# Graph filter convolution on one core: places of the sorted chunks, the engine that writes the early bias, and the step in which a sorted chunk's store is issued

## The chip, the core and the metric

The kernel runs on one NeuronCore of a Trainium2 chip. The metric is the device time of one execution in microseconds (us). The core's engines run their own instruction streams side by side and wait for each other through semaphores: TensorE (PE, with its weight loads as PEld), VectorE (DVE), ScalarE (ACT), GpSimd (POOL) and SyncE (SP). In this kernel SP issues the plain DMAs and POOL the indirect ones.

## The reference

There are 12,500 nodes with 128 features and 412,500 edges, sorted by their destination. Cut to what matters:

```python
h = jnp.maximum(_layernorm(x, axis=-1), 0.0)
h = h @ W_in2f
Wij = ssp(f_ij @ W_f1 + b_f1) @ W_f2 + b_f2          # ssp(x) = softplus(x) - log 2
Wij = Wij * rcut_ij[:, None]
x_ij = h[idx_j] * Wij                                 # idx_j = dst, sorted
agg = jax.ops.segment_sum(x_ij, idx_i, num_segments=h.shape[0])   # idx_i = src, not sorted
out = ssp(agg @ W_o1 + b_o1) @ W_o2 + b_o2
return x + out
```

For each edge a small network of two layers makes a filter of 128 numbers from 20 edge features; the filter, scaled by the edge's cutoff, is multiplied with the row of `h` at one end of the edge, and the products are added up at the other end.

## The kernel before

**Chunks and steps.** The edges are worked in 806 chunks of 512, each with four tiles of 128 edges; four chunks form a group. The main loop runs one `step(k)` (L1521) per chunk, software-pipelined: each step has a list of parts, and a part works for a chunk some steps ahead or behind. The order of the parts is the string `ORDER`, written by hand; since every engine takes its instructions in the order in which they are issued, this string sets the order on each engine:

```python
ORDER, FIRST_ORDER = "EMTBCKHVSPIWJZRLU", "MTBHVPWENISLJZRU"
```

What the parts that matter here do in step k:

- E (`hidden_end`, L875, DVE): ends the first filter layer of chunk k+2; it reads what ACT's last two activations of that layer made.
- M (`message`, L1047 and L1048, DVE): `o` = filter times picked rows, for chunk k. Then the scatter of the chunk before is issued.
- T, B, C, K (DVE): the reduction of ranks, comparisons by which a scatter slot is found, comparisons for the sums.
- H (`picked`, L1034, ACT, four activations): takes the picked rows of chunk k+1 out of their PSUM bank, scaled by the cutoff, as `hg`.
- V (`value`, L997, PE): the second filter layer of chunk k+1, four float32 matmuls into a PSUM bank `v` that holds the bias already.
- S (L1146, PE): pieces of the sums over an earlier segment's messages.
- P (`pick`, L1018, PE): picks the rows of `h` of chunk k+2 by four matmuls with a 0/1 matrix.
- I (`bias`, L989, ACT): writes the bias of the second filter layer into a free `v` bank, for chunk k+2, all 512 columns by one activation.
- Z (`hidden`, L862, or L858 for a sorted chunk, PE): the first filter layer of chunk k+4.
- R (`rank`, L932 and L904, PE): counts by which the messages find free slots.
- L (`hidden_log`, L868, L477, L478, ACT): the first filter layer's softplus for chunk k+3.
- U: remembers TensorE's last matmul of the step (`kept["mm"]`) as the step's signal.

`covered` (L671) makes a step's first scaled pick on ACT, its message on DVE and the scatters wait for the signal of the step before. Three PSUM banks `v` go round in a first-in-first-out list, `v_free`: a pick's bank is returned when ACT has read it (H), a value's when the message has been made (M). `behind` (L682) makes PE's matmuls of chunk k wait for the scatters of chunk k-15, because the message tiles `o` are a ring of 15.

**Two ways for a message to reach its sum.** An ordinary chunk scatters its message by four indirect DMAs of POOL (L1065), one per tile, into slots of its segment; the segments have 352, 176, 120, 56, 56, 32 and 14 chunks, and when one has ended, its slots are loaded and summed while the next ones run. The 63 chunks in `SORT` (L42) do without: a presort, `sorting()` (L1216), a part of which runs beside each early step, sorts their edges by the summing end, from step 18 on and five steps per chunk. Such a chunk needs no ranks, no block comparison and no window; it has three more loads (L843, L844, L847), and its message goes to the DRAM buffer `s_msgs` by one DMA of SP, of 258 KB (L1058, in `scatter`). After the last of them, chunk 553, POOL gathers these rows (`Gather`, L1200).

**The bias** `bf12` is one row of 128 numbers, the same on all partitions, spread over the four tiles by `spread(bf12, QT)`.

Of the kernel before, what the change touches and what calls it, by code (L numbers as in the profile page):

```python
# [10 lines left out]
BF16 = mybir.dt.bfloat16  # L11
F16 = mybir.dt.float16
I32 = mybir.dt.int32
AF = mybir.ActivationFunctionType
# [3 lines left out]
P = 128  # L18
TG = 16
CH = 512  # L20
NCHUNK = TG * P // CH
QT = CH // P
# [16 lines left out]
EPS = 1e-5  # L39
FIRST = 64  # L40
NEAR = 2 * P
SORT = tuple(range(57, 57 + 8 * 63, 8))  # L42
NS = len(SORT)
GR = 6
GJ = 6
# [4 lines left out]
PRE = 18  # L50
# [7 lines left out]
def gnn_kernel(  # L58
# [24 lines left out]
    nc = tc.nc  # L83
# [19 lines left out]
    class Segment:  # L103
# [4 lines left out]
        def __init__(self, k):  # L108
# [7 lines left out]
            n = self.c1 - self.c0  # L116
            kept = n - sum(self.c0 <= k < self.c1 for k in SORT)
            mean = (n * CH - (own[1] - own[0])) * kept / n / QT * P / N
# [21 lines left out]
    def sbuf(name, shape, dtype=F32):  # L140
        return const.tile(shape, dtype, name=name)

    def spread(t, n):
        return t[:, None, :].to_broadcast([t.shape[0], n, P])
# [9 lines left out]
    for q in range(NQ):  # L154
        start = max(0, q * QN - NEAR)
# [25 lines left out]
    bf12 = sbuf("bf12", [P, P])  # L181
# [6 lines left out]
    pick2 = sbuf("pick2", [P, 2], BF16)  # L188
    wst = sbuf("wst", [63, 3, P], BF16)
    idx = sbuf("idx", [P, NBLK], I32)  # L190

    h3 = tc.dram_tile([NTILE * P, 3 * P], BF16, name="h3")
    h3_t = [tc.dram_tile([r, 3 * P], BF16, name=f"h3_{i}") for i, (_, r) in enumerate(tables)]
# [4 lines left out]
    s_msgs = tc.dram_tile([NS * CH + GR, RW], F32, name="s_msgs")  # L198
    segs = [Segment(k) for k in range(len(SEGS))]
# [413 lines left out]
    with tc.tile_pool(name="edge", bufs=2) as edge, tc.tile_pool(  # L613
# [4 lines left out]
        kept = {}  # L618
# [49 lines left out]

        puts = {}

        def covered(inst, back=0):  # L671

            if len(sigs) > back + FREE:
                tc.add_manual_dep(inst.ins, sigs[-1 - back].ins.name,
                                  mybir.DependencyInfo(mybir.DependencyClass.Sync,
                                                       mybir.DependencyReason.DATA),
                                  reason="one signal of TensorE for all of a step")
            return inst
# [90 lines left out]
        class Group:  # L769
# [40 lines left out]
            def rows(self, c):  # L810
# [4 lines left out]
                t = table_of[k]  # L815
                if k in SORT:
                    self.near[c] = self.near[c - 1]
                    self.sorted_load(c, SORT.index(k))
                    return
# [58 lines left out]
            def blocks(self, c):  # L878
                while self.g > 0 and not hasattr(self.cols, "place"):
                    next(self.cols.work)  # L880
                if self.g * NCHUNK + c in SORT:
                    return
# [9 lines left out]
            def rank(self, c):  # L892

                seg = self.seg
                if c == 0:
                    self.top = edge.tile([P, TG], F32, name="top")
                    self.slot = edge.tile([P, TG], I32, name="slot", bufs=8)
                    for i in range(1, NCHUNK):
                        if self.g * NCHUNK + i in SORT:
                            nc.vector.memset(self.top[:, i * QT:(i + 1) * QT], BIG)  # L900
# [84 lines left out]
            def bias(self, c):  # L985


                v = v_free.pop(0)
                nc.scalar.activation(v, spread(bf12, QT), AF.Copy)  # L989
                return v  # L990

            def value(self, c, v):
# [58 lines left out]
            def scatter(self, c, after=None):  # L1051

                views = self.seg.views
                o = self.o.pop(c)
                k = self.g * NCHUNK + c
                if k in SORT:
                    s = SORT.index(k)
                    store = nc.sync.dma_start(  # L1058
                        s_msgs[s * CH:(s + 1) * CH, :].rearrange("(t p) f -> p t f", p=P), o)
                    puts[k] = [store.ins.name] * QT  # L1060
                    return
                names = puts[k] = []
                for i in range(LAST if self.g * NCHUNK + c == NCH - 1 else QT):
                    j = c * QT + i
                    put = nc.gpsimd.indirect_dma_start(  # L1065
                        out=views[j % VIEWS],
                        out_offset=bass.IndirectOffsetOnAxis(ap=self.slot[:, j:j + 1], axis=0),
                        in_=o[:, i, :],
                        in_offset=None,
                    )  # L1070
                    names.append(put.ins.name)
                    if i == 0 and after is not None:
                        tc.add_manual_dep(
                            put.ins, after.ins.name,
                            mybir.DependencyInfo(mybir.DependencyClass.Sync,
                                                 mybir.DependencyReason.DATA),
                            reason="pace of TensorE")
                    if i == 0 and self.g * NCHUNK + c == self.seg.cleared:
                        for name in self.seg.clears:
                            tc.add_manual_dep(  # L1080
                                put.ins, name,
                                mybir.DependencyInfo(mybir.DependencyClass.Sync,
                                                     mybir.DependencyReason.DATA),
                                reason="cleared slots")
# [131 lines left out]
        def sorting():  # L1216
# [5 lines left out]
            def room(name, ring, n):  # L1222
                shape = [P, UT, RW] if ring == "m" else [P, UT, P]
                t = edge.tile(shape, F32, name=name, tag=ring, bufs=n)
                return t.rearrange("p t f -> p (t f)")

            ra, rb, rc, *rp = (room(f"pre{i}", "m", 7) for i in range(5))
            rd = [room(f"pre_d{i}", "to", 5) for i in range(2)]
# [19 lines left out]
            w3 = room("pre_w", "to", 5)  # L1248
# [38 lines left out]
            w = w3[:63, :P]  # L1287
            for i in range(3):
                nc.vector.tensor_copy(wst[:, i, :], w)
                if i < 2:  # L1290
                    nc.vector.tensor_sub(w, w, wst[:, i, :])
            yield
            e = top
            nc.vector.tensor_scalar(e[:, 0:1], pidx, float(SF + 20), None, op0=ALU.is_equal)
# [42 lines left out]
            for s in range(NS):  # L1337
                i = s // SB3
# [15 lines left out]
                for t in range(QT):  # L1354
# [3 lines left out]
                                 skip_group_check=True)  # L1358
                for t in range(QT - 1):
# [4 lines left out]
                        start=False, stop=False, skip_group_check=True)  # L1364
# [6 lines left out]
                                 start=False, stop=True, skip_group_check=True)  # L1371
# [102 lines left out]
        def part(name, upto, make):  # L1474

            for j in range(made.get(name, -1) + 1, min(upto, NCH - 1) + 1):
                make(*of(j))
                made[name] = j
# [42 lines left out]
        def step(k, units=(), order=None):  # L1521
# [95 lines left out]
            for j in range(max(groups) + 1, min(k + LG, 2 * k + 8) // NCHUNK + 1):  # L1617
                group(j)
            part("rows", min(k + LW, kept.get("rows", NCH)), rows)
            if units:  # L1620
                need = turns[units[-1]]
                while kept["load"] < len(order_of) and kept["load"] <= need + AHEAD:
                    live = sum(len(c.m) for c in collects_in)
                    if live >= MB and kept["load"] > need:
                        break
                    c, u = order_of[kept["load"]]
                    c.load(u)
                    kept["load"] += 1
# [33 lines left out]
        t0, i = 8, 0  # L1662
        while i < len(segs):
# [5 lines left out]
            t0, i = due[j], j + 1  # L1669
# [21 lines left out]
        pos, k = 0.0, 0  # L1691
        jobs = {}
        for i, c in enumerate(collects_in):
            for u, (_, nb, _, nt) in enumerate(c.units):
                n = nb * nt
                for j in range(n):
                    pos = max(pos, at[i])
                    k = max(k, next(k for k, t in enumerate(clock) if t > pos) if pos < clock[-1]
                            else len(clock) + int(pos - clock[-1]))
# [333 lines left out]
```

## Time and profile before

| what | value |
|---|---|
| median of three runs | 5026.52 us (5008.05 to 5042.99) |
| the profiled execution's own time | 5043.17 us |
| its span | 5041.5 us |
| granted TensorE clock, mean | 0.872 |
| HBM read, written | 499.23 MB, 404.35 MB |
| message of chunk 30, 352, 370, 553, 805 (start, DVE L1048) | 202.8, 2011.9, 2111.8, 3170.0, 4897.3 us |

Between the last and the first of these times lie the steps; in front of chunk 30 stand the layer norm, the first projections and the start of the pipeline, behind chunk 805 the last sums and the output network.

How to read the views: a group's row names the line, the engine, the operation, out<-in, the count; then the busy time in us and the mean ns of one; then the engine's idle time just before these instructions, and what ended most of it. A row of waits names the waiting engine and line, after the arrow what it waited for, and total us, times, longest us. "issue" is time without a cause that the profile shows, "remote" an event whose sender it cannot name. A row of windows gives from:to and the length, then the busy time of each engine that has instructions there, their counts in brackets, the granted TensorE clock, the DMA engines' busy share and GB/s.

### The profile page before, as it was taken

What the parts mean: (1) busy time and instruction counts of PE and PEld (TensorE: products, weight loads), DVE (VectorE), ACT (ScalarE), POOL (GpSimd) and SP (SyncE); (2) the same over time, 40 slices, a digit from 0 to 9 for tenths busy, and PEclk for the clock granted to TensorE, in tenths of its full rate; (3) what the DMA queues carried; (4) which work ended last, traced back from release to release, by engine and by line L of the source; (5) the groups of instructions that cost most, each with busy time, mean ns of one, the idle gap of its engine ahead of it and who ended that gap; (6) DMA issues with size and microseconds to landing.
All of it is one profiled execution on the core that took longest, in us unless ns stands there. A gap on an engine that the chain in (4) does not pass through costs nothing.

```text
span 5041.5 us, 74193 instructions
## 1 busy us (share of the span) xinstructions
PE 3750.9 (74%) x23450; PEld 2879.7 (57%) x23450; DVE 3419.5 (68%) x8271; ACT 3122.7 (62%) x6868; POOL 3011.8 (60%) x3168
## 2 busy tenths in 40 slices
PE   5666666666666666688887888788877778788889
PEld 3444444444444444466766666666756666667667
DVE  6776766666566666666766676677755557778777
ACT  6676776777666666666666666555544445556543
POOL 5666665656556666655655565555666666556653
PEclk8878888888788778899989998999988889999999
DMA  4556665556444455566676666676645555566658
GB/s 151 159 169 190 181 186 159 169 165 174 133 116 130 127 158 159 158 212 190 207 239 208 193 209 188 194 237 196 203 147 166 177 168 195 179 222 209 194 166 228
DMA packets 570277, 908.76 MB, mean 180 GB/s; under 512 B 159720, under 2 KB 349174, under 8 KB 569876
## 3 DMA queue, kind: packets, MB, share of 16 engines
q1 hardware_dynamic: 465702, 668.16, 44.5%
q0 software_dynamic: 102912, 235.26, 14.3%
q8 instruction: 187, 3.06, 0.3%
q14 instruction: 214, 1.75, 0.1%
q10 hardware_dynamic: 1262, 0.52, 0.0%
HBM read 499.23 MB, written 404.35 MB: 179 GB/s over the span
## 4 chain that ended last, share of the span: by engine, by line


## 5 line engine op out<-in xcount | busy, mean ns | idle before, releaser
L1065 POOL DMA_INDIRECT slots<-o,slot x2971 | 2863.2, 964 | 1847.7 <-issue 749.2
L1034 ACT ACTIVATE hg<-v,rcut 128x128 f32<-128x128 f32 x2972 | 847.5, 370 | 1245.4 <-PE counts L904 598.2
L1146 PE MATMUL sums<-to,m 128*128 128x128 f32 x8716 | 1175.1, 293 | 81.1 <-issue 48.1
L1146 PEld LDWEIGHTS sums<-to,m 128*128 128x128 f32 x8716 | 1126.3, 209 | 103.7 <-issue 60.4
L997 PE MATMUL v<-wf,r 128*128 128x128 f32 x6448 | 1028.5, 307 | 97.5 <-issue 83.2
L997 PEld LDWEIGHTS v<-wf,r 128*128 128x128 f32 x6448 | 978.0, 220 | 211.8 <-issue 155.7
L1048 DVE TENSOR_TENSOR o<-v,hg 128x512 f32<-128x512 f32 x806 | 553.4, 687 | 723.7 <-remote 409.1
L862 PE MATMUL z<-f,wf1z 128*128 128x512 f32 x1486 | 928.5, 709 | 29.9 <-issue 22.0
L875 DVE SCALAR_TENSOR_TENSOR r<-z,nbf,a 128x512 f32<-128x512 f32 x806 | 600.6, 745 | 328.4 <-ACT a L478 152.4
L1018 PE MATMUL v<-near,at 126*128 126x128 bf16 x2964 | 324.8, 235 | 670.0 <-DVE o L1048 337.1
L1018 PEld LDWEIGHTS <-at 126*128 126x128 bf16 x2964 | 251.9, 105 | 735.5 <-issue 630.7
L1124 DVE TENSOR_TENSOR to<-counts,m 128x640 f32<-128x640 bf16 (+3 forms) x793 | 602.1, 794 | 89.3 <-DMA m<-slots 62.7
L478 ACT ACTIVATE a<-a,half 128x512 f32<-128x512 f32 x806 | 581.7, 722 | 26.2
L868 ACT ACTIVATE a<-z,bf 128x512 f32<-128x512 f32 x806 | 540.4, 670 | 2.5 <-issue 2.1
L477 ACT ACTIVATE a<-a 128x512 f32<-128x512 f32 x806 | 507.6, 630 | 25.5
L989 ACT ACTIVATE v<-bf 128x512 f32<-128x512 f32 x806 | 484.8, 601 | 25.4
L932 PE MATMUL counts<-inb,rest_of 128*128 128x392 f16 x736 | 276.6, 376 | 291.3 <-DVE to L1124 146.2
L912 DVE TENSOR_REDUCE top<-counts 128x4 f32<-128x392 f32 x743 | 411.8, 554 | 24.4 <-remote 14.0
L904 PEld LDWEIGHTS <-after 128*128 128x128 f16 x743 | 79.3, 107 | 592.6 <-issue 592.6
L884 DVE TENSOR_TENSOR inb<-counts,blk 128x392 f16<-128x392 bf16 x743 | 411.9, 555 | 0.0
L904 PE MATMUL counts<-inb,after 128*128 128x392 f16 x743 | 282.5, 380 | 15.3 <-issue 12.8
L862 PEld LDWEIGHTS z<-f,wf1z 128*128 128x128 f32 x1486 | 258.7, 217 | 44.1 <-issue 35.7
(227 smaller groups left out, 2480.5 us busy)
## 6 DMA issues: line engine op xcount, KB each, us to landing
rel<-rel_d SPq DMA_DIRECT2D x201, 504.0 KB
m<-slots SPq DMA_DIRECT2D x278, 322.5 KB
m<-slots SPq DMA_DIRECT2D x209, 387.0 KB
m<-slots SPq DMA_DIRECT2D x291, 258.0 KB
f<-in_f_t SPq DMA_DIRECT2D x100, 512.0 KB
slots<-o,slot POOLq DMA_INDIRECT x2971
slots<-zero SPq DMA_DIRECT2D x100, 387.0 KB
slots<-zero SPq DMA_DIRECT2D x58, 516.0 KB
```

The source lines that it names most:

```text
L477: nc.scalar.activation(a, a, AF.Exp, scale=-1.0)
L478: nc.scalar.activation(a, a, AF.Ln, bias=half, scale=0.5)
L862: kept["mm"] = nc.tensor.matmul(z_ps[k % 2], wf1z[:, k, :], self.f, start=True, stop=True)
L868: nc.scalar.activation(self.a[k], z_ps[k % 2], AF.Abs, bias=bf1)
L875: nc.vector.scalar_tensor_tensor(self.r[k], z_ps[k % 2], nbf1, self.a.pop(k), op0=ALU.max, op1=ALU.add)
L997: mm = nc.tensor.matmul(v[:, i, :], r[:, i * P:(i + 1) * P], wf2, start=False, stop=True, skip_group_check=True)
L1018: mm = nc.tensor.matmul(ps[:, i, :], at[:, i * P:(i + 1) * P], near, start=i == 0, stop=i == QT - 1, skip_group_check=True)
L1034: act = nc.scalar.activation(hg[:, i, :], ps[:, i, :], AF.Copy, scale=cut[:, i:i + 1])
L1048: covered(nc.vector.tensor_mul(o[:, :, :P], v, hg))
L1065: put = nc.gpsimd.indirect_dma_start(out=views[j % VIEWS], out_offset=bass.IndirectOffsetOnAxis(ap=self.slot[:, j:j + 1], axis=0), in_=o[: ...
L1124: nc.vector.tensor_tensor(to[:, :n, :], count_ps[:, None, :].to_broadcast([P, n, P]), m[:, :n, P:].to_broadcast([P, n, P]), op=ALU.is_equal)
L1146: kept["mm"] = nc.tensor.matmul(self.acc[b // QT][:, i, :], m[:, j, :P], to[:, j, :], start=t == 0, stop=t == self.seg.tiles(b) - 1)
```

## The change

It has three parts.

1. **The sorted chunks' places** (L42). Before, they were every eighth chunk from 57 to 553. Now 44 stand seven apart from 57 on and 19 ten apart from 373 on, each moved back to the second chunk of its group (4·(x//4)+1): 57, 65, 69, 77, 85, 93, 97, ..., 345, 349, 357, 373, 381, 393, 401, 413, ..., 541, 553. Number and last place are the same. Of chunks 30 to 351, 43 are sorted now and 37 were before; of 352 to 367 one and two; of 368 to 553 nineteen and twenty-four.
2. **The bias of chunks 30 to 351** is written by TensorE: one matmul of a 128x128 matrix of ones (a weight load of `ones_b`, spread) with `bias_w`, 128x512 in bf16, that starts the bank; `value` adds to it as before. `bias_w` holds the bias as three bf16 numbers that add up to it, on partitions 0, 32 and 64, zeros elsewhere. Two more pieces of `sorting()` make it, some ten small DVE operations. Chunks before 30 and from 352 on keep the activation.
3. **The store of a sorted chunk** is kept in a list, `stores`, and issued by a later step, once three steps have gone by, right after that step's loads of rows.

```diff
-SORT = tuple(range(57, 57 + 8 * 63, 8))
+SORT = tuple(4 * (x // 4) + 1 for x in [57 + 7 * i for i in range(44)] + [373 + 10 * i for i in range(19)])
...
+    bias_w = sbuf("bias_w", [P, P], BF16)
+    ones_b = sbuf("ones_b", [P, 1], BF16)
...
+        stores = []
+
+        def store():
+
+            k, o = stores.pop(0)
+            s = SORT.index(k)
+            put = nc.sync.dma_start(
+                s_msgs[s * CH:(s + 1) * CH, :].rearrange("(t p) f -> p t f", p=P), o)
+            puts[k] = [put.ins.name] * QT
...
                 v = v_free.pop(0)
-                nc.scalar.activation(v, spread(bf12, QT), AF.Copy)
+                k = self.g * NCHUNK + c
+                if PRE + 12 <= k < segs[0].c1:
+                    kept["mm"] = nc.tensor.matmul(v, ones_b.to_broadcast([P, P]),
+                                                  spread(bias_w, QT), start=True, stop=False,
+                                                  skip_group_check=True)
+                else:
+                    nc.scalar.activation(v, spread(bf12, QT), AF.Copy)
                 return v
...
                 if k in SORT:
-                    s = SORT.index(k)
-                    store = nc.sync.dma_start(
-                        s_msgs[s * CH:(s + 1) * CH, :].rearrange("(t p) f -> p t f", p=P), o)
-                    puts[k] = [store.ins.name] * QT
+                    stores.append((k, o))
                     return
...
+            yield
+            t, w = rd[1][:, :P // 2].bitcast(BF16), w3[:, :P]
+            nc.vector.memset(bias_w, 0.0)
+            nc.vector.memset(ones_b, 1.0)
+            nc.vector.tensor_copy(t, bf12)
+            nc.vector.tensor_copy(bias_w[0:1, :], t[0:1, :])
+            nc.vector.tensor_sub(w, bf12, t)
+            yield
+            nc.vector.tensor_copy(t, w)
+            nc.vector.tensor_copy(bias_w[32:33, :], t[32:33, :])
+            nc.vector.tensor_sub(w, w, t)
+            nc.vector.tensor_copy(bias_w[64:65, :], w[64:65, :])
             yield
...
             part("rows", min(k + LW, kept.get("rows", NCH)), rows)
+            while stores and stores[0][0] <= k - 3:
+                store()
```

With the added lines the numbers of the changed program are higher: L997 becomes L1015, L1018 becomes L1036, L862 becomes L874, L932 and L904 become L944 and L916, L1034 becomes L1052, L868, L477 and L478 become L880, L479 and L480, L1058 becomes L679.

The first place is PE's order in an early step, from the values of one chunk (`v<-wf,r`) over the picks of the next (`near`, `at`) to the hidden layer (`z<-f,wf1z`) and the rank (`counts`). Before:

```order
L997 MATMUL v_159<-wf_63,r 128x128 x3
L1018 LDWEIGHTS at [waits DMAHW1_49,DVE_49]
L1018 MATMUL v_160<-near,at 128x128 [waits DVE_49]
...
L1018 MATMUL v_160<-near,at 128x128
L862 MATMUL z_154<-f,wf1z 128x512
L932 LDWEIGHTS rest_of
L932 MATMUL counts<-inb,rest_of 128x392 [waits DVE_49]
L904 LDWEIGHTS after
L904 MATMUL counts<-inb,after 128x392
```

and now:

```order
L1036 LDWEIGHTS at [waits DMAHW1_49,DVE_49]
L1036 MATMUL v_162<-near,at 128x128 [waits DVE_49]
...
L1036 MATMUL v_162<-near,at 128x128
L1003 LDWEIGHTS ones_b
L1003 MATMUL v_160<-bias_w,ones_b 128x512 [waits Activation_49]
L874 MATMUL z_156<-f,wf1z 128x512
L944 LDWEIGHTS rest_of
L944 MATMUL counts<-inb,rest_of 128x392 [waits DVE_49]
L916 LDWEIGHTS after
L916 MATMUL counts<-inb,after 128x392
```

A weight load and a matmul of 128x512 now stand between the picks and the hidden layer, and the matmul waits for ACT.

The second place is ACT's order over two early steps: scaled picks (`hg`), bias (`v<-bf`), the softplus of the hidden layer (`a`). Before:

```order
L1034 ACTIVATE hg<-v_159,rcut 128x128 [waits DVE_49]
L1034 ACTIVATE hg<-v_159,rcut 128x128 x3
L989 ACTIVATE v_159<-bf_84 128x512 [waits Activation_49]
L868 ACTIVATE a<-z_154,bf_66 128x512
L477 ACTIVATE a<-a 128x512 [waits Activation_49]
L478 ACTIVATE a<-a,half 128x512 [waits Activation_49]
L1034 ACTIVATE hg<-v_158,rcut 128x128 [waits DVE_49,PE_49]
```

and now:

```order
L1052 ACTIVATE hg<-v_162,rcut 128x128 [waits DVE_49,PE_49]
L1052 ACTIVATE hg<-v_162,rcut 128x128 x3
L880 ACTIVATE a<-z_156,bf_66 128x512
L479 ACTIVATE a<-a 128x512 [waits Activation_49]
L480 ACTIVATE a<-a,half 128x512 [waits Activation_49]
L1052 ACTIVATE hg<-v_161,sorted 128x128 [waits DMAHW4_49,DVE_49,PE_49]
```

The activation that wrote the bias is gone from between them; nothing else of the step's six-line pattern moved.

## The prediction

> **What bounds the kernel now.** I read the page's busy times and costliest groups first, because they say which engine could be the bound.
>
> ```profile
> span 5041.5 us, 74193 instructions
> PE 3750.9 (74%) x23450; PEld 2879.7 (57%) x23450; DVE 3419.5 (68%) x8271; ACT 3122.7 (62%) x6868; POOL 3011.8 (60%) x3168
> ...
> L1065 POOL DMA_INDIRECT slots<-o,slot x2971 | 2863.2, 964 | 1847.7 <-issue 749.2
> ...
> L875 DVE SCALAR_TENSOR_TENSOR r<-z,nbf,a 128x512 f32<-128x512 f32 x806 | 600.6, 745 | 328.4 <-ACT a L478 152.4
> ...
> L989 ACT ACTIVATE v<-bf 128x512 f32<-128x512 f32 x806 | 484.8, 601 | 25.4
> ```
>
> No engine is full: the busiest, PE, works 74% of the span. So the program is a ring of engines that wait for each other, and what an edit is worth must be read stage by stage. I cut the span where the edits cut it: from the message of chunk 30 to that of 352 (202.8 to 2011.9 us), from that of 370 to that of 553 (2111.8 to 3170.0), and the rest, with the short piece before 352 by itself, when the presort of the sorted chunks is over. First the windows of the scatters' line L1065 alone (instructions in brackets), then the windows of all engines.
>
> ```profile
> core 0: us, POOL busy (x), PEclk, DMA share, GB/s
> 202.80:2011.90 1809.10, 1100.65 (x1141) 0.82 0.55 159
> 1888.00:2011.90 123.90, 77.93 (x80) 0.83 0.54 160
> 2111.80:3170.00 1058.20, 614.28 (x640) 0.92 0.66 206
> 3170.00:4897.30 1727.30, 969.25 (x1007) 0.90 0.60 189
> ```
>
> ```profile
> 202.80:2011.90 1809.10, 1193.73 (x6444) 794.50 (x6443) 1188.17 (x3356) 1264.73 (x2876) 1100.65 (x1141) 0.82 0.55 159
> ...
> 2111.80:3170.00 1058.20, 870.69 (x5946) 713.83 (x5945) 728.57 (x1594) 687.74 (x1490) 614.28 (x640) 0.92 0.66 206
> ```
>
> A chunk that is not sorted costs four scatters, a sorted one none. Divided by four, the counts are 285.25, 20, 160 and 251.75 unsorted chunks, so one costs 6.34, 6.20, 6.61 and 6.86 us in the four stretches. These lie within 11% of each other, though the second table (busy PE, PEld, DVE, ACT, POOL) shows PE at 66% of its time early and 82% in the middle, and sorted chunks are one in eight in the first and the third stretch and none in most of the last. A step's time thus goes with the scatters and not with PE's load. Why they do not come faster, the waits of the early stretch show (what waited for what, total, times, longest).
>
> ```profile
> POOL slots L1065 <- issue: 298.8, 956, 1.5
> PE v L1018 <- DVE o L1048: 297.9, 108, 8.1
> POOL slots L1065 <- remote: 149.3, 81, 2.6
> POOL slots L1065 <- PE counts L904: 145.7, 36, 7.9
> ACT hg L1034 <- remote: 82.2, 33, 4.8
> DVE o L1048 <- remote: 76.7, 39, 4.0
> DVE r L875 <- ACT a L478: 73.5, 51, 5.8
> ACT hg L1034 <- PE counts L904: 35.5, 23, 3.5
> DVE r L875 <- ACT a L477: 34.3, 23, 2.5
> PEld v L997 <- ACT v L989: 10.9, 12, 1.6
> ```
>
> One scatter takes 1100.65/1141 = 0.965 us and 298.8/956 = 0.313 us of issue between two, so four take 5.1 us of the 6.34. The missing 1.2 us is POOL waiting for TensorE's end-of-step signal: 36 times plainly (L904 is its last matmul), 81 times as "remote", the same instruction held for an event that the profile cannot name. That signal closes a ring: message (DVE, L1048), picks of the next chunk but one (PE, L1018), hidden layer, rank (L904), signal, next message and scatters.
>
> **The sorted chunks' places.** Their number, 63, and the last, 553, stay. Of chunks 30 to 351 six more are sorted (43 for 37), of 352 to 367 one fewer, of 368 to 553 five fewer. By the prices above this is −6 × 6.34 = −38.0 us early and 6.20 + 5 × 6.61 = +39.3 us later, together **+1 us**. If the price of the six differs by as much as the lowest and the highest do (6.20, 6.86), it is −4 to +4 us. What a step saves in PE work by being sorted counts nothing here, because PE's load did not set the step. The last scatter is still that of chunk 805 and the gathers still begin after 553.
>
> **The bias, taken from ACT.** For chunks 30 to 351, 322 of them, L989 goes: 322 × 0.601 = 193.5 us of ACT's 1264.7 in that stretch. What of it can reach the path? In ACT's order L989 stands between the scaled picks (L1034) and the three activations of the hidden layer, whose last two end what DVE's L875 waits for: 51 + 23 = 74 waits, 107.8 us. Each can come at most 0.601 us earlier, so 74 × 0.601 = **−44 us**. Behind the waiting L875 stand the message and everything else of DVE's step, so I count it in full, though some of it could end at the signal instead. The value matmuls' waits for L989, 10.9 us, also go, but lie in the same steps; I add none. The bounds: 0, if each of these waits is followed by one for the signal, and −108, if earlier steps keep ACT ahead and all 74 waits vanish.
>
> **The bias, given to TensorE.** Added are 322 matmuls of 128x512 in bf16, each with a weight load. The trace has no such instruction with 128 rows; the nearest rows of the early stretch are these (mean ns of one behind the busy time).
>
> ```profile
> L904 PE MATMUL counts<-inb,after 128*128 128x392 f16 x284 | 116.5, 410 | 0.0
> L1382 PE MATMUL sums<-pre,pre_d 128*107 128x512 bf16 x249 | 70.8, 410 | 0.0
> L858 PE MATMUL z<-sorted,wst 63*128 63x512 bf16 x114 | 44.4, 513 | 1.8 <-issue 1.8
> L904 PEld LDWEIGHTS <-after 128*128 128x128 f16 x284 | 32.9, 116 | 120.2 <-issue 120.2
> ```
>
> The presort's L1382 has 128 rows and 512 columns too: 410 ns from start to end, of which 70.8/249 = 284 are its own, since four follow each other and overlap; L858 gives 513. I take 0.410 us, as the new one stands alone; the loads, 0.116, overlap other matmuls. PE gets 322 × 0.41 = 132 us more, 11% of its 1193.7. The new matmul stands between the picks and the hidden layer, so it is inside the ring, and it waits for ACT's L1034 to have emptied its bank: hidden layer, rank and signal queue behind it. Where the scatters wait for L904 plainly, it costs its full time: 36 × 0.41 = **+15 us**. Bounds: 0, if PE finds it in the 34% of idle time, as the middle stretch suggests, where PE has 4.73 us of work for each message (870.69/184) against 3.71 early (1193.73/322) at nearly the same price for a scatter; and 322 × (0.410 + 0.116) = +169, if each early step is as tight as that.
>
> **The stores, three steps later.** A sorted chunk's message leaves by one SP DMA, L1058. What SP waited:
>
> ```profile
> SPq L1110 <- PE counts L904: 861.7, 179, 13.5
> ...
> SPq L1058 <- DVE o L1048: 47.0, 7, 9.0
> ```
>
> The store held SP's queue 7 times, 47 us in all; behind it stood loads for steps ahead, and none of the compute groups above names a load of SP among what it waited for. SP waits many times as long for other things. I take **0**, bounds −47 and 0; the message tiles are a ring of 15, so holding one three steps longer blocks nothing. The some ten new DVE operations, which split the bias once, are at most 10 × 0.745 = 7 us by L875's row, in the presort's gaps: 0. The presort ends two steps later, at about step 345, still ahead of its reader.
>
> **The sum:** 5043.2 (the profiled execution's own time) + 1 − 44 + 15 + 0 = 5015, that is −28 us. The median of the runs shown, 5026.52, is 16.7 us under the profiled execution, and the predicted time is the median less 28: **4998 us**, −0.6%. About 1% is what a measurement of this kernel can tell from no change.
>
> **The rivals.** (a) *ACT's relief spreads.* With 0.6 us less per step ACT is ahead, and all waits for the logs go: −108 + 15 + 1 = −92, 4934 us. For it speaks that ACT is the busiest engine early (1264.73 of 1809.10, 70%); against it, that the middle stretch, with 3.74 us of ACT's work per message (687.74/184) against 3.93 early, is not cheaper.
>
> (b) *The new matmul lengthens the ring: slower.* One mechanism: the signal goes out later, by the matmul, its load, and where L1034 starts late, by the wait for it. The place is PE between picks and hidden layer. It decides as soon as the signal and not the logs is what a step waits for last; the "remote" rows of POOL count as signals too, then: 117 of 285 unsorted steps are tight, so 322 × 117/285 = 132 steps by 0.526 us, +70, and the 44 are not gained: 5026.5 + 70 + 1 = 5097 us. For it: 117 waits on POOL, and 56 late starts of L1034. Against: the middle stretch's heavier PE.
>
> (c) *Scatters pace everything.* The 743 unsorted chunks are as many as before, and what holds POOL up is not what PE and ACT do between signals: 5026.5 + 1 = 5028 us. For it: prices within 11% over stages whose loads differ by more; the unnamed "remote" events. Against: the 145.7 us with a plain releaser.
>
> (d) *PE's clock rises.* PE's granted clock is 0.82 early and 0.92 in the middle, where it is busier. If its added work brings the early clock to 0.92, its old 1193.7 us shrink by 1193.7 × (1 − 0.82/0.92) = 130 us, 7% of the stretch; by the share of tight steps (36 to 117 of 285) 16 to 53 us reach the path, beside the forecast: 4945 to 4982, I take 4965. Against: the clock differs between stages that differ in much else, and 11% more work brings PE only to 73%.
> [...]
>
> **How the numbers follow.** Forecast 0.34 (of it 0.24 within 1%, 0.10 beyond), (a) 0.24, (b) 0.19 (0.17 slower by over 1%, 0.02 within), (c) 0.15, (d) 0.08. Faster by over 1%: 0.10 + 0.24 + 0.08 = 0.42; within: 0.24 + 0.02 + 0.15 = 0.41; slower: 0.17. The forecast's own range, from −44 and 0 to 0 and +15, with the spread of the three runs (17 us each way), is 4966 to 5058. For 8 in 10 I reach down to (a) with all that the stores could save, 4934 − 47 = 4887, and up to (b), 5097; what is left out is half of (b) and a gain beyond (a).
>
> **What would show it.** Right: in the early stretch L989 is gone and a PE group of 322 128x512 matmuls stands there at about 410 ns; DVE's waits for the activations of the logs fall from 107.8 to some 64 us; POOL's waits for TensorE's last matmul rise by some 15 us; the time from the message of 30 to that of 352 falls by some 67 us (38 of it by places, 29 by the bias) and from 352 to 553 rises by 39. It would be wrong if the early stretch with its six fewer unsorted chunks gains less than 38 us (then (b)), if DVE's waits for the logs all but vanish and the early price falls under 6.1 us per unsorted chunk (then (a)), or if the middle stretch changes by another amount than its scatters.

## The result: slower by 1.4%

The changed kernel takes 5091.56 us (median of four runs, 5081.61 to 5107.99), the kernel before 5021.4 in the same comparison (four runs, 5008.05 to 5042.99): a ratio of 1.0139, 95% interval 1.0092 to 1.0185. It is 70 us slower where 28 less were forecast. Its profiled execution took 5107.99 us. From its page:

```profile
span 5106.3 us, 74561 instructions
PE 3797.0 (74%) x23772; PEld 2909.1 (57%) x23772; DVE 3423.7 (67%) x8280; ACT 2922.7 (57%) x6546; POOL 3011.9 (59%) x3168
...
L1080 POOL DMA_INDIRECT slots<-o,slot x2971 | 2863.5, 964 | 1904.9 <-issue 743.6
```

The work moved as planned: ACT is busy 200 us less, PE 46 more, and POOL's 2971 scatters cost the same. The span grew by 65 us, and so did POOL's idle time before its scatters, by 57 (1904.9 after 1847.7).

The same stretches as before, between the same messages (30 to 352 and 370 to 553), first the scatters' line alone, then all engines:

```profile
200.50:2043.60 1843.10, 1077.91 (x1116) 0.84 0.55 157
2145.50:3216.30 1070.80, 633.50 (x660) 0.91 0.66 203
```

```profile
200.50:2043.60 1843.10, 1228.26 (x6752) 811.72 (x6752) 1179.12 (x3341) 1066.08 (x2552) 1077.91 (x1116) 0.84 0.55 157
```

(The five times given for the kernel before are ends of its messages, 0.7 us behind their starts; the lengths are not touched by that.) The early stretch became 34 us longer although it has 25 scatters fewer: 1843.1/279 = 6.61 us per chunk that is not sorted, after 6.34. The middle one has 20 more and is 13 longer; the piece between the two is 2 longer, and what follows chunk 553 some 18. Where the early time went, the waits of that stretch show (a selection, longest first):

```profile
POOL slots L1080 <- PE counts L916: 177.7, 49, 7.4
DVE o L1066 <- remote: 117.8, 45, 5.7
POOL slots L1080 <- remote: 113.8, 69, 2.3
ACT hg L1052 <- remote: 103.4, 25, 6.3
ACT hg L1052 <- PE counts L916: 89.0, 43, 6.5
POOL slots L1080 <- PE sums L1395: 63.8, 13, 12.3
DVE r L887 <- ACT a L480: 60.7, 43, 5.0
PE v L1003 <- issue: 52.2, 55, 4.0
PE v L1003 <- ACT hg L1052: 43.4, 37, 7.3
```

DVE waits less for ACT's logs, as forecast. But PE now stands before its new matmul for 96 us (52.2 + 43.4), 43.4 of them for ACT's picks. The picks wait longer for the rank and for unnamed events (192.4 us after 117.7), and so do the messages for unnamed ones (117.8 after 76.7). The scatters wait no longer for these two together (32 us more for the rank, 36 less for unnamed events), but longer for the presort's matmuls, L1395 above all (63.8; before, the same matmul at L1368 held them for 22.0).

### The profile page after: what moved, and what is told of

It is laid out like the page before. It is cut to its first block, busy times and chain, and to the rows that moved or that the text cites. A ratio compares the mean times of both kernels' runs of the same rounds, so it can differ in the third digit from the quotient of the medians.

```text
span 5106.3 us, 74561 instructions
## 1 busy us (share of the span) xinstructions
PE 3797.0 (74%) x23772; PEld 2909.1 (57%) x23772; DVE 3423.7 (67%) x8280; ACT 2922.7 (57%) x6546; POOL 3011.9 (59%) x3168
## 4 chain that ended last, share of the span: by engine, by line
## 5 line engine op out<-in xcount | busy, mean ns | idle before, releaser
L1080 POOL DMA_INDIRECT slots<-o,slot x2971 | 2863.5, 964 | 1904.9 <-issue 743.6
L1052 ACT ACTIVATE hg<-v,rcut 128x128 f32<-128x128 f32 x2972 | 845.2, 369 | 1348.4 <-PE counts L916 700.2
L1015 PE MATMUL v<-wf,r 128*128 128x128 f32 x6448 | 1021.4, 305 | 90.8 <-issue 83.2
L1015 PEld LDWEIGHTS v<-wf,r 128*128 128x128 f32 x6448 | 968.7, 218 | 207.1 <-issue 158.2
L874 PE MATMUL z<-f,wf1z 128*128 128x512 f32 x1486 | 886.8, 679 | 44.7 <-issue 30.8
L1036 PE MATMUL v<-near,at 126*128 126x128 bf16 x2964 | 311.8, 229 | 588.4 <-DVE o L1066 336.0
L1036 PEld LDWEIGHTS <-at 126*128 126x128 bf16 x2964 | 244.7, 103 | 655.8 <-issue 585.1
L480 ACT ACTIVATE a<-a,half 128x512 f32<-128x512 f32 x806 | 581.8, 722 | 26.2
L880 ACT ACTIVATE a<-z,bf 128x512 f32<-128x512 f32 x806 | 553.0, 686 | 5.9 <-PE z L874 3.5
L479 ACT ACTIVATE a<-a 128x512 f32<-128x512 f32 x806 | 507.7, 630 | 25.6
L944 PE MATMUL counts<-inb,rest_of 128*128 128x392 f16 x736 | 273.6, 372 | 294.7 <-DVE to L1139 146.8
L916 PEld LDWEIGHTS <-after 128*128 128x128 f16 x743 | 78.1, 105 | 586.5 <-issue 586.5
L874 PEld LDWEIGHTS z<-f,wf1z 128*128 128x128 f32 x1486 | 275.0, 210 | 153.2 <-issue 126.3
L1007 ACT ACTIVATE v<-bf 128x512 f32<-128x512 f32 x484 | 291.1, 601 | 15.2
L916 PE MATMUL counts<-inb,after 128*128 128x392 f16 x743 | 280.2, 377 | 19.6 <-issue 16.2
```

The costliest lines, as they stand in the source:

```text
L479: nc.scalar.activation(a, a, AF.Exp, scale=-1.0)
L480: nc.scalar.activation(a, a, AF.Ln, bias=half, scale=0.5)
L874: kept["mm"] = nc.tensor.matmul(z_ps[k % 2], wf1z[:, k, :], self.f, start=True, stop=True)
L880: nc.scalar.activation(self.a[k], z_ps[k % 2], AF.Abs, bias=bf1)
L1015: mm = nc.tensor.matmul(v[:, i, :], r[:, i * P:(i + 1) * P], wf2, start=False, stop=True, skip_group_check=True)
L1036: mm = nc.tensor.matmul(ps[:, i, :], at[:, i * P:(i + 1) * P], near, start=i == 0, stop=i == QT - 1, skip_group_check=True)
```

## The experiments

The runs came on different chips, and these differ more than any edit. On most of them the kernel before takes 5.0 to 5.1 ms, as at first; on one it takes 4.36. The expectations call them the slow chips and the fast chip. Each run is compared with the kernel before on its own chip. The differences in us are those of the medians; the ratios, with their 95% intervals, are worked out apart, and the two can differ by some us. The expectations weigh three theories of the 70 us: TensorE's bias matmul lengthens the ring (1), the places cost the time (2), or the late stores do (3).

### The three parts alone, and the bias at another place (fast chip, before 4355 us)

The places alone are the first hunk of the diff, the bias alone the hunks of `bias` and `sorting`, the stores alone the rest. The fourth kernel is the bias alone with the matmul moved to `value`; against the kernel with the bias alone, cut:

```diff
                 v = v_free.pop(0)
-                    kept["mm"] = nc.tensor.matmul(v, ones_b.to_broadcast([P, P]),
...
             def value(self, c, v):
...
+                if PRE + 12 <= k + 1 < segs[0].c1:
+                    nc.tensor.matmul(v, ones_b.to_broadcast([P, P]), spread(bias_w, QT),
+                                     start=True, stop=False, skip_group_check=True)
                 for i in range(QT):
```

The places:

> Only the sorted chunks' places are changed; the bias stays on ACT and the stores stay where they were. Theory 1 (TensorE's bias matmul lengthens the ring of picks, hidden layer, rank and signal): the places are worth nothing, within 10 us of before: about 38 us off between the messages of chunks 30 and 352 and 39 us on between 352 and 553. Theory 2 (the places cost the time): +40 to +70 us, most of it after chunk 352, where the changed kernel has 30 us more than before. Theory 3 (the late stores): nothing here.

The bias:

> Only the bias of chunks 30 to 351 goes to TensorE. Theory 1: +60 to +80 us, all of it between the messages of chunks 30 and 352, and ACT's picks stand ahead of some 40 us of TensorE's waits for its new matmul. Theory 2: the forecast's own gain shows, -44 and +15, about -28 us. Theory 3: as theory 2.

The stores:

> Only the stores of the sorted chunks are issued three steps later. Theories 1 and 2: within 10 us of before. Theory 3 (a store that now stands behind the loads of later steps holds message tiles or SP's queue longer, or meets other transfers): +30 us or more.

The bias ahead of the values:

> As the kernel with the bias alone, but TensorE's bias matmul stands directly ahead of the value matmuls of the same chunk, one step later, where its bank has been empty for a step: it waits for no pick of ACT, and the picks and the hidden layer are not parted by it. Theory 1 in the form that the wait for ACT does the harm: most of the +70 us goes, and the gain of 28 us may show. Theory 1 in the form that TensorE's own 0.4 to 0.5 us in each step does it: as slow as the bias alone, within 15 us. Theory 2: -28 us, as for the bias alone.

Measured: places 4340.55 us (0.9960, 0.9935 to 0.9986), -15; bias 4337.12 (0.9953, 0.9934 to 0.9972), -18; stores 4386.59 (1.0065, 1.0042 to 1.0088), +31; bias ahead of the values 4307.73 (0.9892, 0.9858 to 0.9927), -47. Theories 1 and 2 failed here: neither bias nor places lost time. Only the stores did, by about what theory 3 had said. The last kernel gained more than any theory said.

### The whole change on the fast chip, and the bias taken apart

Two kernels take the bias edit to pieces. One leaves the bias of chunks 30 to 351 out; the value matmuls start their banks:

```diff
-                nc.scalar.activation(v, spread(bf12, QT), AF.Copy)
+                if not PRE + 12 <= k < segs[0].c1:
+                    nc.scalar.activation(v, spread(bf12, QT), AF.Copy)
...
-                                          start=False, stop=True, skip_group_check=True)
+                                          start=PRE + 12 <= k + 1 < segs[0].c1, stop=True, skip_group_check=True)
```

The other keeps ACT's bias and has TensorE run one more matmul ahead of the hidden layer:

```diff
+                    if PRE + 14 <= self.g * NCHUNK + k < segs[0].c1 + 2:
+                        nc.tensor.matmul(z_ps[k % 2], ones_b.to_broadcast([P, P]),
+                                         spread(bias_w, QT), start=True, stop=True)
```

The kernel before, for its trace:

> The kernel before, unchanged, for its trace on the chip of this call, where it needed 4355 us instead of 5021 if it is the chip of the first four runs. All theories: within 0.5% of the other runs of before here. If the difference between the chips lies in when TensorE's end-of-step signal reaches the other engines, the waits that the profile calls remote are all but gone (over 500 us in the first trace); if it lies in the DMA transfers alone, they stay.

The whole change:

> The changed kernel, unchanged. If the three parts add up as in the first four runs (places -17, bias -20, later stores +31 us): within 10 us of before on the same chip. If the parts act on each other (more sorted chunks early make the late stores or the early bias dearer): +40 to +70 us, as where it was first measured.

No bias:

> The places and the stores are those of before. For chunks 30 to 351 nobody writes the bias: the value matmuls start their banks themselves, so these chunks' filters lack the bias. This is ACT's relief of 193 us without TensorE's work. Theory 1 (the new matmul costs what the relief gains): -45 to -70 us against before, at least 25 us faster than the bias alone (-20). If the matmul at its new place costs nothing: -20 us, as the bias alone.

The extra matmul:

> The places and the stores are those of before and ACT writes the bias as before; in the same 322 early steps TensorE runs one more matmul of 128x512 of the same operands just ahead of the hidden layer, into the hidden layer's own bank, which that then overwrites. This is TensorE's added work without ACT's relief and without a wait for ACT. Theory 1 (TensorE's time in the ring counts): +30 to +130 us. If TensorE has room for it: within 10 us of before.

Measured: before 4352.63; the whole change 4338.71 (0.9957, 0.9940 to 0.9974), -18; no bias 4328.46 (0.9931, 0.9907 to 0.9954), -28; the extra matmul 4364.85 (1.0020, 1.0005 to 1.0035), +8. So on this chip ACT's relief is worth 28 us, TensorE's matmul costs 8, and the two make 20, near the 18 of the bias alone. Theory 1 had wanted more of both (45 to 70 gained, 30 to 130 lost). The three parts alone add up to -2 (-15, -18, +31), the whole change to -18. The expectation for adding up, within 10 us, was missed; with intervals of some 10 us for each part, that they act on each other is not shown. The whole change gains there about what the forecast said, 0.4% for 0.6%, but this is luck: its terms were +1, -44, +15 and 0, and measured are -15, -28, +8 and +31.

What differs between the chips, the waits of the early stretch of the kernel before show on the fast one, all rows over 1 us for the scatters, the messages and the scaled picks that name the rank or the hidden layer:

```profile
POOL slots L1065 <- PE counts L904: 67.4, 37, 6.0
ACT hg L1034 <- PE counts L904: 66.6, 33, 5.3
ACT hg L1034 <- PE z L862: 5.0, 4, 2.6
DVE o L1048 <- PE counts L904: 2.2, 5, 0.8
```

No wait of this trace is called remote, while in the first trace of the same program those of POOL, ACT and DVE for an unnamed event were among the largest (149.3, 82.2 and 76.7 us early). What such a wait is, a stretch of the timeline of before on the first chip shows, in order of start (start, duration, engine, line):

```profile
1402.30 0.33 PE L904 MATMUL counts<-inb,after 128*128 128x392 f16 x1
...
1402.80 0.42 PE L1360 MATMUL sums<-pre,ones 128*128 128x294 f16 x3
...
1403.58 0.72 ACT L478 ACTIVATE a<-a,half 128x512 f32<-128x512 f32 x1
1404.33 0.75 DVE L875 SCALAR_TENSOR_TENSOR r<-z,nbf,a 128x512 f32<-128x512 f32 x1 [1.75 <-issue]
...
1406.05 0.96 POOL L1065 DMA_INDIRECT slots<-o,slot  x1 [0.30 <-issue]
...
1409.17 0.69 DVE L1048 TENSOR_TENSOR o<-v,hg 128x512 f32<-128x512 f32 x1 [4.01 <-remote]
1409.27 0.17 ACT L1365 ACTIVATE nall<-sums 98x1 f16<-98x1 f32 x1 [4.97 <-remote]
...
1409.92 0.58 PE L1018 MATMUL v<-near,at 126*128 126x128 bf16 x4 [5.75 <-DVE o L1048]
...
1413.25 0.96 POOL L1065 DMA_INDIRECT slots<-o,slot  x1 [6.24 <-PE counts L904]
```

TensorE's signal matmul ends at 1402.63 and the presort's next at 1403.2. Yet the message that waits for the one and ACT's `nall` that waits for the other start together at 1409.2, 2.2 us after the last scatter of a batch has ended (1407.0). This is the common picture there: between chunks 57 and 352 POOL works in batches, mostly of four or eight scatters 1.27 us apart, with 145 pauses between them, and its next batch comes 1.95 us after the last scatter's end in the median. Of the 194 early waits of DVE and ACT for an unnamed event, 144 end 1.5 to 2.5 us after a scatter's end, while POOL stands idle; 18 end while a scatter runs, and none ends later than 2.5 us, though POOL's pauses are up to 11 us long. On the fast chip POOL has 40 such pauses for 145, and its batches run on over many chunks. The starts of the scatters, worked out for neighbouring chunks (first start of the next, less last start of the one before, less 1.27 us):

| kernel, chip | pause between neighbours, chunks 57 to 351 | pause across a sorted chunk, 57 to 351 | the same two, 370 to 552 |
|---|---|---|---|
| before, first chip | 222 x 0.76 us | 36 x 4.53 us | 138 x 1.11, 23 x 4.16 |
| changed, first chip | 210 x 0.83 | 42 x 5.04 | 146 x 1.07, 19 x 4.39 |
| before, fast chip | 222 x 0.22 | 36 x 1.14 | 138 x 0.32, 23 x 2.00 |
| changed, fast chip | 210 x 0.20 | 42 x 1.37 | 146 x 0.22, 19 x 0.93 |

This is what the prediction missed. On the first kind of chip a sorted chunk is not free: it makes the scatters pause for 4.5 us, 3.8 more than between neighbours, against the 5.8 us (four scatters and a pause of 0.76) that an unsorted one costs. On the fast chip it costs about one.

The chips differ in TensorE's clock too. The early stretch of the kernel before on the fast one:

```profile
164.00:1698.00 1534.00, 1076.86 (x6447) 726.88 (x6446) 1184.14 (x3356) 1255.73 (x2877) 1099.18 (x1136) 0.89 0.66 187
```

The granted clock is 0.89 there for 0.82, and the same matmuls keep PE busy for 117 us less (1193.7 on the first chip), against a stretch that is 275 us shorter. Whether the clock is higher because the pauses are short, or the other way round, no run here decides.

### Two further versions (a slow chip, before 5101 us)

The new places with the bias matmul ahead of the values, and the stores five steps behind (`k - 5` for `k - 3` in the changed line).

> The new places, the stores as before, and TensorE's bias matmul directly ahead of the value matmuls as in the run that was best so far (-47 us). If the gains add up: -17 - 47, about -64 us. If the sorted chunks and the bias save the same idle time: no more than -47.

> Only the stores of the sorted chunks are later, by five steps instead of three; places and bias as before. Three steps later the store fell into the first step of a group of four, where the loads of a group's edge features and window rows are issued too; five steps later it falls into the third. If what cost 31 us is the meeting with those loads: within 10 us of before. If it is the lateness, by which the stores come nearer to the sums' loads or hold the message tiles: +31 us or more.

Measured: 5116.53 (1.0029, 1.0009 to 1.0049), +16, and 5102.88 (1.0017, 0.9997 to 1.0037), +2. The first expectation was made for the fast chip and is not tested by this. The second result lies where the meeting with a group's loads would have it, but it doesn't decide: it was not run on the chip on which three steps cost 31, and on a slow chip three steps cost so little (1.0029 below) that the intervals overlap.

### The parts on a slow chip (before 5037 us)

> The places alone, a second time. On the fast chip they gained 17 us. Theory 1 (on the slow chip each break of the scatters, about 167 of them between chunks 30 and 352, is one trip round the ring and pays TensorE's new work): within 20 us of before. Theory 2 (the places cost the time): +40 us or more.

> The bias alone, a second time. On the fast chip it gained 20 us. Theory 1: on a slow chip +50 to +80 us (167 breaks, longer by 0.3 to 0.5 us each), all before chunk 352. Theory 2: within 20 us of before or faster.

> The changed kernel, a second time. On a slow chip +50 to +80 us, as at first; on the fast one -18 us, as there. If it is neither, the first result hung on more than these two kinds of chip.

> The early chunks without any bias, a second time: ACT is relieved and TensorE does nothing more. Theory 1: on a slow chip within 20 us of before, since a break is a trip through TensorE, DVE and the scatters and ACT's bias is not on it. If ACT's bias is on it: -40 to -100 us.

Measured: places 5073.31 (1.0072, 1.0049 to 1.0096), +37; bias 5059.98 (1.0038, 1.0020 to 1.0056), +23; the whole change 5095.47 (1.0130, 1.0103 to 1.0156), +59; no bias 5034.01 (0.9993, 0.9976 to 1.0011), nothing. So the first result comes back on another chip of its kind, and 37 + 23 = 60 makes it up. Theory 1 had the bias two to three times too large and the places wrong. Theory 2 missed both by 3 us (40 or more for the places, within 20 for the bias), inside the intervals, so it is nearer; but the bias is a cost of its own.

The scatters' windows of the kernel without the early bias, which takes the time of before, and then of the places alone, both between the same messages (30 to 352, 370 to 553, 553 to 648):

```profile
200.50:2018.20 1817.70, 1100.17 (x1140) 0.82 0.55 158
2113.50:3153.20 1039.70, 616.39 (x641) 0.92 0.68 210
3153.20:3810.80 657.60, 360.04 (x374) 0.91 0.62 193
```

```profile
200.30:2010.50 1810.20, 1082.38 (x1117) 0.81 0.56 160
2111.80:3184.90 1073.10, 635.09 (x660) 0.91 0.66 203
3184.90:3856.20 671.30, 362.08 (x376) 0.89 0.59 187
```

Early, 23 scatters fewer save 29 us (at 1.27) and the pauses between neighbours fall by 35 (from 222 x 0.83 to 210 x 0.71), but the pauses across sorted chunks grow from 161 us in all (36 x 4.46) to 211 (42 x 5.02). That would leave 14 us; the stretch as a whole, which begins ahead of the sorted chunks, became 7.5 shorter. The middle stretch is longer by 33 us, as forecast: 24 for its 19 more scatters and 13 more between neighbours, and fewer sorted chunks save it nothing, since each of its pauses became longer (88 us in all before, 87 now). After chunk 553 another 14 us came, which nobody had forecast. These are single traces; they differ by 45 us where the medians differ by 39. How the loss is shared out among the stretches differs even between chips of one kind: in the whole change's trace on this chip the early stretch takes 1824.8 us, 7 more than without the bias, and the middle one 1072.2, 33 more, while on the first chip it was 34 and 13.

And ACT's relief: in the kernel without the early bias DVE waits much less for the logs, and the time stays. Its row, to be held against the 73.5 and 34.3 of before on the first chip:

```profile
L877 DVE SCALAR_TENSOR_TENSOR r<-z,nbf,a 128x512 f32<-128x512 f32 x323 | 240.1, 743 | 79.1 <-ACT a L480 51.5 <-issue 17.5 <-ACT a L479 9.6
```

### What of the bias and the places costs (a slow chip, before 5097 us)

The last four kernels repeat three and add one, whose places are

```diff
-SORT = tuple(range(57, 57 + 8 * 63, 8))
+SORT = tuple([4 * (x // 4) + 1 for x in [57 + 7 * i for i in range(44)]] + [409 + 8 * i for i in range(19)])
```

The extra matmul:

> TensorE's extra matmul with ACT's bias kept, a second time (on the fast chip +8 us). On a slow chip, where ACT's relief gave nothing: if TensorE's own time in each break is the cost, about the +23 us of the bias alone; if the wait for ACT's picks is, within 10 us of before.

The bias ahead of the values:

> The bias matmul directly ahead of the value matmuls, a second time (on the fast chip -47 us, the best). On a slow chip, where the values run in the time in which TensorE waits for the message: within 12 us of before, if what costs is the place between the picks and the hidden layer; +23 us, if it is TensorE's added work wherever it stands.

The stores:

> The stores alone, a second time (on the fast chip +31 us, all of it between chunks 370 and 553). On a slow chip, where five steps later gave +9: within 15 us of before, if the breaks of the scatters hide it; +30 us, if it is the same there.

The other late places:

> The new early places to 357, then none to 408, then every eighth from 409 to 553, nineteen in all; bias and stores as before. The counts of sorted chunks in the three stretches are those of the change. On a slow chip: if only the counts matter, +37 us as the places alone; if the last spacing of ten costs the 15 us after 553, some +22, and the stretch 553 to 648 takes no more than with the old places.

Measured: extra matmul 5121.69 (1.0044, 1.0027 to 1.0061), +24; bias ahead of the values 5096.46 (0.9991, 0.9977 to 1.0006), -1; stores 5110.61 (1.0029, 1.0013 to 1.0044), +13; the other late places 5110.73 (1.0030, 1.0014 to 1.0047), +14.

The extra matmul without ACT's relief and without a wait for ACT costs as much as the bias alone: it is TensorE's matmul between picks and hidden layer that costs, 24 us for 322, and neither the wait nor ACT. Moved ahead of the values the same matmul is nearly free, as ACT's relief, which that kernel has too, was worth nothing on a slow chip (0.9993). The rows of the extra matmul, and of the bias ahead of the values:

```profile
L859 PE MATMUL z<-bias_w,ones_b 128*128 128x512 bf16 x320 | 146.9, 459 | 0.0
```

```profile
L1001 PE MATMUL v<-bias_w,ones_b 128*128 128x512 bf16 x320 | 140.3, 438 | 4.9 <-ACT hg L1041 2.9 <-issue 2.0
```

Nearly equal work, 0.46 and 0.44 us. That it is free at the values' place because TensorE then waits for the message anyway is argued: early, its picks wait 305.2 us for messages in that kernel, and 288.0 with the extra matmul.

The spacing of the last sorted chunks doesn't explain the 14 us after 553: with the old spacing of eight there, that stretch takes 673.9 us, against 653.6 (extra matmul) and 661.1 (bias ahead of the values) with the old places; with the old places and the late stores it takes 670.3, so the cause is open. Between 370 and 553 the other late places cost nothing. That stretch of the bias ahead of the values, where everything after chunk 352 is as before, and of the other late places:

```profile
2136.20:3205.90 1069.70, 872.95 (x5957) 721.27 (x5956) 730.88 (x1592) 688.32 (x1489) 616.13 (x640) 0.91 0.66 204
```

```profile
2124.20:3191.60 1067.40, 870.91 (x6033) 716.73 (x6033) 740.32 (x1607) 688.22 (x1489) 635.06 (x660) 0.93 0.66 204
```

Twenty scatters more took no more time, by single traces. So the number of late sorted chunks alone doesn't set what that stretch costs; that their spacing does is likely, but the spacing of ten was not run on this chip, and the 14 us in all here, less than either expectation, can't be held directly against the 37 on another. With the bias ahead of the values, worth nothing here, the new places cost 16 on another slow chip, so their cost may vary by chip too.

## Why the prediction was wrong, point by point

- **The sorted chunks' places, +1: failed, and the largest miss.** The step that failed is "A chunk that is not sorted costs four scatters, a sorted one none", with each stretch's time shared out among the unsorted chunks. It hid in the price of 6.34 what a sorted chunk itself costs: of the 331 us of pauses between chunks 57 and 352 of the first trace, 163 lie at 36 sorted chunks. A chunk that becomes sorted takes away four scatters and the pauses on both sides of it and puts one long pause there: 5.08 + 2 x 0.76 - 4.53 = 2.1 us, so six more early could win 12 us and not 38; 7.5 were measured on the later slow chip. The 39 us to be paid after 352 came on that chip (33, and 6 between 352 and 370), but on the first one 15 (13 and 2), and with the other late places the stretch from 370 on paid nothing; so the price by the count is not sound there either. In all +37 (1.0072) on that chip.
- **ACT's relief, -44: failed.** The waits fell to 63.3 us (60.7 + 2.6), where some 64 were forecast, and the time didn't: without any early bias the ratio is 0.9993. What failed is the step "so I count it in full": what stands behind these waits did not come sooner. The bound "0, if each of these waits is followed by one for the signal" fits the slow chips: in the trace there without any early bias ACT's scaled picks still wait 183.5 us for the rank and unnamed events between the messages of 30 and 352 (56.9 + 126.6), and the messages 120.9 us for unnamed ones. On the fast chip the relief is worth 28 us.
- **TensorE's matmul, +15: right in place, a little small.** +24 by the extra matmul, within the bounds of 0 and 169. That the middle stretch's PE load "did not set the step" was no evidence for a matmul inside the ring.
- **The stores, 0: too small on both kinds of chip.** +13 (1.0029) and +31 (1.0065). The prediction looked at what SP waits for and not at what the moved transfer does to others; that no compute group waits for a load of SP held for the rows that it showed only, for over the whole span of before DVE's `to` (L1124) waits 62.7 us, 54 times, for the loads `m<-slots`. On the fast chip, in the window 1770 to 2700 us, DVE waits longer for the sums' loads; before and then with the later stores:

```profile
DVE to L1124 <- DMA m<-slots: 61.7, 33, 5.5
```

```profile
DVE to L1131 <- DMA m<-slots: 83.7, 27, 5.5
```

  That these loads come later because of the stores is argued from this, not shown apart.
- **The sum.** Measured one by one on slow chips, 37 and 23 us on one and 13 on another make 73; the whole change, +70 and +59. On the chip of the 37 and the 23 the whole is 59, which leaves nothing for the stores; with intervals of some 10 us each, what they add there is open. (The range's upper end leaves out the places' +1.)
- **The rivals.** (b) named the place, the matmul in the ring, but gave it 70 us; it costs a third of that, and that its 5097 lay near the 5092 measured is luck, since the places made up the rest. (c) was right that ACT's relief does not reach the scatters on these chips, and wrong that TensorE's matmul and a moved sorted chunk cost nothing. (a) is refuted there by the run without bias. (d) did not come: with PE busy for 67% of the early stretch (1228.26 of 1843.10 us) after 66%, the granted clock went from 0.82 to 0.84, not to 0.92. That the added work raises it that far was the author's estimate; what sets the clock, no run shows.

No version that keeps the bias beats the kernel before on both kinds of chip beyond the uncertainty. The bias ahead of the values comes nearest: 0.9991 on a slow one, 0.9892 on the fast one.

## What to carry to other kernels

An average per unit over a stretch (here 6.34 us per unsorted chunk) is no price of the unit: before changing how many units of the other kind there are, measure the gap around one of them in the pacing engine's own timeline. Taking work off a busy engine gains only if what waits for it is not released by a later event anyway; ask what the next wait would be. Here the early chunks without any bias gave 0.9993 on a slow chip and 0.9931 on the fast one. And the place in a ring at which work is added counts: here the same matmul cost 24 us between picks and hidden layer and nothing (-1) ahead of the values, where its engine, as argued, waits in any case. A result of about 1% should be taken on more than one chip.

## What the runs showed of the hardware

The same program takes 5.02 to 5.10 ms on some chips and 4.36 on another, 13 to 15% less, at nearly the same scatter time (1100.65/1141 = 0.965 us early on the first, 1099.18/1136 = 0.968 on the fast one). On a slower one other engines stand for several us after the matmul that they wait for has ended by the profile (6.5 in the stretch of the timeline above), and go on together, some 2 us after the last scatter of a batch (144 of 194 such waits at 1.5 to 2.5 us); on the faster one no wait is called remote. We read this as TensorE's signals that come late. What holds them up stayed open: it follows POOL's batches, but no run takes the scatters away. The sign of a change of 1% can hang on this: the same kernel was 1.4% and 1.3% slower on two chips and 0.4% faster on a third.
